# Layer 0 expert tiles: a row's weight, shift and scale chosen on GpSimd in six instructions instead of on VectorE in five

## The chip, the cores and the metric

The kernel runs on one core of one Trainium2 chip. The metric is the device time of one execution in microseconds (us). The time of the kernel before is the median of three runs, 3926.92 us (3926.24 to 3932.78).

## The reference, cut to what matters

The network has two layers. Each is a token mixer (attention with a top-k mask in layer 0, four selective scans in layer 1) followed by a mixture of experts. The change lies in the mixture of experts of layer 0, where each of the 4 x 1024 tokens goes to two of eight experts:

```python
def _moe(tokens, router_w, w1, b1, w2, b2):
    probs = jax.nn.softmax(logits, axis=-1)
    rw, re = jax.lax.top_k(probs, TOP_K)
    rw = rw / jnp.maximum(rw.sum(-1, keepdims=True), 1e-12)
    combine = jnp.zeros((N, E), tokens.dtype).at[jnp.arange(N)[:, None], re].set(rw)
    out = tokens
    for e in range(E):
        h = jax.nn.gelu(tokens @ w1[e] + b1[e], approximate=False)
        y = h @ w2[e] + b2[e]
        out = out + combine[:, e:e + 1] * y
    return out
...
t = _to_tokens(x)
t = t + _L0_ffn_ref(_ln_t(t), ...)
```

The tokens are normalized (`_ln_t`), so the sum for a token is its raw row, plus its normalized row, plus the two experts' results, each times its weight.

## The kernel before, in words

Attention runs first, image by image (about 0 to 1955 us in the profile). As an image is finished, its tokens are routed, and each row of 256 channels is written twice into `slots_x0`, a DRAM buffer with a region for each expert. A row carries five more numbers: at position C (256) the number of its first expert, at C + 1 and C + 2 what gives its weight, at C + 3 the shift and at C + 4 the scale of its normalization.

Then come the layer 0 tiles (about 1955 to 2193 us): 36 tiles of 256 rows, each for one expert. The loop `for i in range(USUAL)` calls seven steps for each tile, in this order:

- `load` (L1442 to L1447): SyncE's DMA queue fetches the rows `xs` (6 buffers) and the expert's weights `w1` and `w2` (4 buffers).
- `normed` (L1454, L1456): `xn`, the normalized rows, two halves of 128. In tiles 0 to 13 GpSimd makes both; from tile 14 on VectorE makes the first half and ScalarE the second.
- `small` (L1470 to L1481): VectorE copies the expert's two biases out of a table at an offset in a register (`b1e`, `b2e`). It then makes three pairs of numbers for the 256 rows. `best` is 1 where the row's first expert is the tile's expert. `wt`, the row's weight, is best times one number plus another. `shift` is best times the row's shift. In the end `best` is overwritten with (scale + 1) times best. Each of these tiles has 2 buffers.
- `turned` (L1463, L1465): TensorE transposes `xn` into `tp` (one PSUM buffer), VectorE copies it to `xe`.
- `hidden` (L1488, L1490): TensorE multiplies by `w1` into `hp` (2 PSUM buffers), ScalarE applies Gelu and the bias and writes `hid`.
- `result` (L1496, L1499): TensorE multiplies by `w2` into `yp` (one PSUM buffer), VectorE adds the bias and writes `ys` (8 buffers).
- `store` (L1503, L1505, L1507): ScalarE makes ys times `wt` plus `shift` in place, VectorE adds the raw row times `best`, and GpSimd starts the DMA that writes the tile to `rows_y0`. In this way the one tile that belongs to a token's first expert also brings its raw and its normalized row.

After each tile, other work is issued six steps at a time (the list `beside`). From tile 14 on this is `whole(0)`: 16 gathers on GpSimd (L1918), which fetch each token's two results from the rows of tiles 0 to 14 (`FIRST` is 15) and add them; they are issued beside tiles 14, 15 and 16. After a pause come their transposes, and then layer 1's first preparation: the normalization (L1805 to L1835), the projections (L1841, L1863) and the step sizes (L1857 to L1892), and `lead`, which has one GpSimd product over 1024 columns (L1958). From tile 22 on `whole(1)` gathers image 1 in the same way (`SECOND` is 23).

No order is written out by hand in this part, unlike in the attention and in the scans, which stand under `manual_schedule`. Here the compiler puts the instructions of each engine into an order of its own, from the code's order, the data that each needs and the buffers that it has to wait for. What is then in an engine's queue is issued in that order. `small` of a tile follows `normed` in the code and stands ahead of the tile's matmuls and of what is issued beside that tile. The buffers tie it to the tile two before: `wt` and `shift` are free again when L1503 of that tile has read them, the last factor when L1505 has.

Of the kernel before, what the change touches and what calls it, by code (L numbers as in the profile page):

```python
# [11 lines left out]
F32 = mybir.dt.float32  # L12
# [5 lines left out]
ALU = mybir.AluOpType  # L18
# [3 lines left out]
P = 128  # L22
B = 4
C = 256
# [15 lines left out]
T = 256  # L40
# [25 lines left out]
def metaformer(ctx: ExitStack, tc: tile.TileContext, t: dict, out: bass.AP):  # L66
    nc = tc.nc
# [120 lines left out]
    every_expert = cons.tile([P, NTILE], F32, tag="every_expert", name="every_expert")  # L188
# [1226 lines left out]
    def tiles_of_0(st, name):  # L1415
# [7 lines left out]
        pb = st.enter_context(tc.tile_pool(name=f"{name}_b", bufs=2))  # L1423
# [5 lines left out]
        class Tile0:  # L1429
# [37 lines left out]
            def small(self):  # L1467
                e = self.register(0, E - 1, [mybir.EngineType.DVE])
                self.b1e = pb.tile([P, CT], F32, tag="b1e", name="b1e")
                nc.vector.tensor_copy(self.b1e, b1[:, bass.ds(e, 1)].rearrange("p o c -> p (o c)"))  # L1470
                self.b2e = pb.tile([P, C], F32, tag="b2e", name="b2e")
                nc.vector.tensor_copy(self.b2e, b2[:, bass.ds(e, 1)].rearrange("p o d -> p (o d)"))
                self.best = pb.tile([P, T // P], F32, tag="best", name="best")
                nc.vector.tensor_scalar(self.best, self.xs[:, :, C], every_expert[:, self.i : self.i + 1], None,
                                        ALU.is_equal)
                self.wt = pb.tile([P, T // P], F32, tag="wt", name="wt")
                nc.vector.tensor_tensor(self.wt, self.best, self.xs[:, :, C + 1], ALU.mult)
                nc.vector.tensor_tensor(self.wt, self.wt, self.xs[:, :, C + 2], ALU.add)
                self.shift = pb.tile([P, T // P], F32, tag="shift", name="shift")
                nc.vector.tensor_tensor(self.shift, self.best, self.xs[:, :, C + 3], ALU.mult)  # L1480
                nc.vector.scalar_tensor_tensor(self.best, self.xs[:, :, C + 4], 1.0, self.best, ALU.add, ALU.mult)  # L1481

            def hidden(self):
                hp = ps_h.tile([P, CT, T], F32, tag="hp", name="hp")
# [16 lines left out]
            def store(self):  # L1501
                for a in range(T // P):
                    nc.scalar.activation(self.ys[:, a], self.ys[:, a], AF.Identity, bias=self.shift[:, a : a + 1],  # L1503
                                         scale=self.wt[:, a : a + 1])
                    nc.vector.scalar_tensor_tensor(self.ys[:, a], self.xs[:, a, :C], self.best[:, a : a + 1],  # L1505
                                                   self.ys[:, a], ALU.mult, ALU.add)
                nc.gpsimd.dma_start(rows_y0[ts(self.i, T)].rearrange("(a p) c -> p a c", p=P), self.ys)  # L1507

# [456 lines left out]
    with ExitStack() as st:  # L1965
        Tile0, pb, ps_n = tiles_of_0(st, "m0")
# [282 lines left out]
    with ExitStack() as st:  # L2249
        pb = st.enter_context(tc.tile_pool(name="m1_b", bufs=2))  # L2250
# [267 lines left out]
```

## Time and profile before

| | us |
|---|---|
| median of three runs | 3926.92 |
| the profiled execution | 3942.8 |
| its span, from the first to the last instruction | 3940.7 |
| TensorE (PE) busy in the span | 3366.7 |
| VectorE (DVE) busy | 3044.7 |
| ScalarE (ACT) busy | 2779.1 |
| GpSimd (POOL) busy | 1969.6 |
| GpSimd's gathers L1918 between 1955 and 2195 us (the 32 of images 0 and 1) | 41.0 |
| GpSimd's stores L1507, 36 of them | 29.7 |
| GpSimd's normalization L1456, 28 halves | 17.9 |

The profile is of one execution, which took 15.9 us longer than the median. In its groups, a row names the line, the engine, the operation, the tile written and the tiles read, with their shapes; then the busy time and the mean duration in ns, and after the next bar the idle time ahead of these instructions. In a timeline a row has the start and the duration in us, then the instruction, and in brackets how long its engine had been idle before it and what it had waited for. Where several instructions are merged into one row, an x and their number stand at its end. PE's matmul ends are modelled, and spans on GpSimd are rough.

### The profile page before, as it was taken

To read this page: it belongs to the slowest core of one execution; us is meant where nothing else is said; L and a number is where in the kernel's file an instruction comes from. 1 tells how busy PE (TensorE), PEld (TensorE's weight loads), DVE (VectorE), ACT (ScalarE), POOL (GpSimd) and SP (SyncE) were. 2 spreads that over 40 slices of the span, in tenths; PEclk is the share of its full clock that TensorE was granted. 3 is DMA by queue.
4 is the path that set the end of the run, shared out by engine and by line. 5 is a ranking of instruction groups with operands and counts; after the bars stand their busy time and mean duration, and the time that the engine had idled before them with its cause. 6 is when DMAs were issued, how large, how long until landed. Compare 5 with 4: busy or idle time off the path is not lost. (4 is left out here: it accounts for less than half of the span.)

```text
span 3940.7 us, 49978 instructions
## 1 busy us (share of the span) xinstructions
PE 3366.7 (85%) x17139; PEld 1891.0 (48%) x17186; DVE 3044.7 (77%) x5283; ACT 2779.1 (71%) x3756; POOL 1969.6 (50%) x1796
## 2 busy tenths in 40 slices
PE   8378888888888888886688889998998989998998
PEld 5134444534344444543375433443443433687887
DVE  3689898998989898989476789999999999331113
ACT  2889999899989999997244677767767777322223
POOL 0145544585647564675443576556556558213112
PEclk9567887788778787787798999999999999999999
DMA  9400084000000000000275344334334334556666
GB/s 294 111 1 1 1 233 126 1 1 25 17 1 1 1 28 6 1 12 12 80 230 158 127 126 129 125 106 131 121 106 131 124 106 150 162 182 195 198 205 232
DMA packets 279802, 393.74 MB, mean 100 GB/s; under 512 B 80368, under 2 KB 221424, under 8 KB 279408
## 3 DMA queue, kind: packets, MB, share of 16 engines
q1 hardware_dynamic: 253824, 333.73, 27.7%
q0 software_dynamic: 21216, 53.73, 4.2%
q10 hardware_dynamic: 4496, 2.97, 0.2%
q8 instruction: 138, 2.26, 0.2%
q14 instruction: 128, 1.05, 0.1%
HBM read 280.41 MB, written 109.94 MB: 99 GB/s over the span
## 5 line engine op out<-in xcount | busy, mean ns | idle before, releaser
L828 POOL TENSOR_SCALAR dr<-s_n,last 128x1024 bf16<-128x1024 f32 x250 | 719.0, 2892 | 735.2 <-DVE state L856 377.1
L738 ACT ACTIVATE junk_a<-s_n,state 128x1024 int8<-128x1024 f32 x448 | 514.7, 1149 | 23.8 <-DVE low L859 6.5
L2114 POOL TENSOR_TENSOR da_c<-prod,come 128x1024 f32<-128x1024 f32 x128 | 257.7, 2013 | 369.6 <-DVE h L2120 321.8
L742 DVE TENSOR_SCALAR_CACHE_REDUCE junk_v<-s_n,state 128x1024 int8<-128x1024 f32 x320 | 408.7, 1277 | 8.8
L2314 ACT ACTIVATE hid<-hp,b 128x256 f32<-128x256 f32 x288 | 120.2, 470 | 350.0 <-issue 231.0
L789 DVE SCALAR_TENSOR_TENSOR w<-s_n,win 128x1024 f32<-128x1024 f32 x256 | 350.3, 1369 | 5.3
L2323 DVE TENSOR_TENSOR ys<-yp,b2e 128x512 f32<-128x512 f32 x36 | 24.9, 692 | 383.8 <-PE yp L2320 383.8
L792 DVE MAX8 win<-w 128x8 f32<-128x1024 f32 x256 | 314.5, 1228 | 8.8
L2125 PE MATMUL sum<-h,ident 128*128 128x512 f32 x512 | 264.1, 640 | 56.7 <-DVE h L2120 52.9
L896 ACT ACTIVATE ex<-sT 128x1024 f32<-128x1024 f32 x256 | 247.0, 1016 | 91.7 <-PE sT L888 91.7
L2103 DVE TENSOR_TENSOR_SCAN sum<-da,uu 128x1024 f32<-128x1024 f32 x127 | 289.6, 2280 | 27.5 <-PE sum L2085 13.9
L2079 POOL TENSOR_TENSOR uu<-dx,bb 128x1024 f32<-128x1024 f32 x127 | 303.6, 2391 | 1.7 <-DMA bb<-bc_d 1.7
L738 ACT ACTIVATE junk_a<-s_n,guess 128x1024 int8<-128x1024 f32 x256 | 294.3, 1150 | 7.2
L2096 DVE TENSOR_TENSOR_SCAN h<-da,uu 128x1024 f32<-128x1024 f32 x127 | 287.9, 2267 | 1.0 <-POOL uu L2079 1.0
L2120 DVE TENSOR_TENSOR_SCAN h<-da_c,uu 128x1024 f32<-128x1024 f32 x127 | 288.3, 2270 | 0.0
L2091 PE MATMUL sum<-da_c,ident 128*128 128x512 f32 x512 | 257.1, 626 | 33.1 <-POOL da_c L2114 29.0
L906 PE MATMUL o_ps<-ex,vT 128*32 128x256 f32 x2048 | 236.9, 450 | 51.4 <-ACT ex L896 36.7
L2325 POOL DMA_INDIRECT results<-ys,to x72 | 70.2, 974 | 415.0 <-DVE ys L2323 359.8
L2063 ACT ACTIVATE da_c<-delta,a_log 128x1024 f32<-128x1024 f32 x128 | 269.5, 2106 | 5.2 <-DMA rows_y<-ys 5.2
L2310 PE MATMUL hp<-xe,w 128*128 128x256 f32 x1152 | 259.9, 384 | 8.9 <-ACT hid L2314 5.3
L2320 PE MATMUL yp<-w2e,hid 128*128 128x256 f32 x1152 | 257.8, 382 | 11.3 <-issue 11.3
L772 ACT COPY s_n<-sp 128x1024 f32<-128x1024 f32 x256 | 245.2, 1003 | 19.1 <-PE sp L764 11.5
(796 smaller groups left out, 7568.8 us busy)
## 6 DMA issues: line engine op xcount, KB each, us to landing
cb<-bc_d SPq DMA_DIRECT2D x128, 512.0 KB
bb<-bc_d SPq DMA_DIRECT2D x127, 512.0 KB
w<-in_w SPq DMA_DIRECT2D x36, 1024.0 KB
w2e<-in_w SPq DMA_DIRECT2D x36, 1024.0 KB
slots_x<-zeros SPq DMA_DIRECT2D x1, 33669.0 KB
slots_x<-zeros SPq DMA_DIRECT2D x1, 33282.0 KB
w<-in_w SPq DMA_DIRECT2D x72, 256.0 KB
xs<-slots_x SPq DMA_DIRECT2D x36, 261.0 KB
```

The source lines that it names most:

```text
L738: nc.scalar.activation(junk, self.row(r), AF.Sign, bias=thr, scale=-1.0, accum_out=u)
L742: nc.vector.tensor_scalar(junk, self.row(r), thr, None, ALU.is_lt, ALU.add, accum_out=u)
L789: nc.vector.scalar_tensor_tensor(w, self.row(r), self.win[:, r, 0:1], self.row(r), ALU.is_gt if r < LAST_DVE else ALU.is_ge, ALU.subtract, ...
L792: nc.vector.max(out=self.win[:, r, 1:], in_=w)
L828: ins = eng.tensor_scalar(dr, self.row(r), self.last[:, r : r + 1], None, ALU.is_lt)
L2063: nc.scalar.activation(grid(self.da_c), cols_flipped(self.prep.delta[:, self.c]), AF.Exp, scale=self.decay)
L2079: nc.gpsimd.tensor_tensor(self.uu[:, 0], self.prep.dx[:, self.c], self.bb, ALU.mult)
L2096: nc.vector.tensor_tensor_scan(rows.rearrange("p r w -> p (r w)"), self.da, self.uu[:, 0], 0.0, ALU.mult, ALU.add)
L2103: nc.vector.tensor_tensor_scan(self.sum[:, ::-1], self.da[:, ::-1], self.uu[:, 0][:, ::-1], 0.0, ALU.mult, ALU.add)
L2120: nc.vector.tensor_tensor_scan(self.hs, self.da_c, self.uu[:, 1], 0.0, ALU.mult, ALU.add)
L2125: nc.tensor.matmul(cols_flipped(self.sum[:, ts(h, HALF)]), ident, grid(self.hs)[:, :, ts(h, half)], start=False, stop=False)
L2310: nc.tensor.matmul(hp[:, i], self.w1[:, c, ts(2 * r + i, P)], self.xe[:, c], start=(c == 0), stop=(c == CT - 1))
```

## The change

The three values of a row are made by GpSimd. The comparison, the two operations for `wt` and the one for `shift` are the same, on another engine. The last one, (scale + 1) times best, is made in two operations, scale times best and then plus best, and goes to a tile of its own, `scale`, also with 2 buffers; L1505 reads it instead of `best`. The two bias copies stay on VectorE. `best` is now read by GpSimd alone.

```diff
@@ small
-                self.best = pb.tile([P, T // P], F32, tag="best", name="best")
-                nc.vector.tensor_scalar(self.best, self.xs[:, :, C], every_expert[:, self.i : self.i + 1], None,
+                pool = nc.gpsimd.tensor_tensor
+                self.best, self.wt, self.shift = (pb.tile([P, T // P], F32, tag=n, name=n) for n in ("best", "wt", "shift"))
+                nc.gpsimd.tensor_scalar(self.best, self.xs[:, :, C], every_expert[:, self.i : self.i + 1], None,
                                         ALU.is_equal)
-                self.wt = pb.tile([P, T // P], F32, tag="wt", name="wt")
-                nc.vector.tensor_tensor(self.wt, self.best, self.xs[:, :, C + 1], ALU.mult)
-                nc.vector.tensor_tensor(self.wt, self.wt, self.xs[:, :, C + 2], ALU.add)
-                self.shift = pb.tile([P, T // P], F32, tag="shift", name="shift")
-                nc.vector.tensor_tensor(self.shift, self.best, self.xs[:, :, C + 3], ALU.mult)
-                nc.vector.scalar_tensor_tensor(self.best, self.xs[:, :, C + 4], 1.0, self.best, ALU.add, ALU.mult)
+                pool(self.wt, self.best, self.xs[:, :, C + 1], ALU.mult)
+                pool(self.wt, self.wt, self.xs[:, :, C + 2], ALU.add)
+                pool(self.shift, self.best, self.xs[:, :, C + 3], ALU.mult)
+                self.scale = pb.tile([P, T // P], F32, tag="scale", name="scale")
+                pool(self.scale, self.best, self.xs[:, :, C + 4], ALU.mult)
+                pool(self.scale, self.scale, self.best, ALU.add)
@@ store
-                    nc.vector.scalar_tensor_tensor(self.ys[:, a], self.xs[:, a, :C], self.best[:, a : a + 1],
+                    nc.vector.scalar_tensor_tensor(self.ys[:, a], self.xs[:, a, :C], self.scale[:, a : a + 1],
                                                    self.ys[:, a], ALU.mult, ALU.add)
```

The same functions serve a rare branch with more tiles than usual (`more_tiles`); the profile shows none of it.

## The prediction

> **What bounds the kernel now.** I read the page first (busy shares, then the chain of work that ended last), then the stage of the layer 0 tiles by itself: busy time by stretches, groups of instructions, waits, and the timeline of all engines and of GpSimd alone. The chain on the page starts at 2190.36 us with the last store of a layer 0 tile (2.55 us to land); the loads of the next stage follow it. So the end of this stage, 1955 to 2193 us, is on the path, and each microsecond that it grows or shrinks reaches the end. Inside it:
>
> ```profile
> 1980.00:2018.00 38.00, 35.95 (x172) 28.97 (x171) 28.64 (x103) 15.87 (x33) 18.72 (x27) 1.00 0.79 235
> 2018.00:2055.00 37.00, 31.57 (x148) 24.86 (x147) 25.18 (x86) 17.38 (x37) 13.08 (x14) 1.00 0.76 222
> 2055.00:2080.00 25.00, 22.88 (x112) 17.85 (x111) 19.96 (x64) 12.12 (x25) 16.34 (x15) 1.00 0.99 282
> ...
> 2120.00:2150.00 30.00, 17.84 (x67) 13.41 (x66) 25.42 (x58) 17.41 (x23) 5.16 (x4) 0.78 0.37 117
> ```
>
> The columns after the length are the busy times of PE, PE's weight loads, VectorE (DVE), ScalarE (ACT) and GpSimd (POOL). Up to 2080 us TensorE is the fullest (35.95 of 38 us, 22.88 of 25); only from 2120 to 2150 us does VectorE lead, with 25.42 of 30 us. Tiles 3 to 9 come every 4.34 us, tiles 10 to 20 every 4.82 us (two in 9.63).
>
> The five operations that the change takes from VectorE:
>
> ```profile
> L1474 DVE TENSOR_SCALAR best<-xs,every_expert 128x2 f32<-128x2 f32 x36 | 9.1, 251 | 0.2
> L1477 DVE TENSOR_TENSOR wt<-best,xs 128x2 f32<-128x2 f32 x36 | 8.6, 238 | 0.8
> L1478 DVE TENSOR_TENSOR wt<-wt,xs 128x2 f32<-128x2 f32 x36 | 5.7, 158 | 0.0
> L1480 DVE TENSOR_TENSOR shift<-best,xs 128x2 f32<-128x2 f32 x36 | 5.7, 159 | 0.0
> L1481 DVE SCALAR_TENSOR_TENSOR best<-xs,best 128x2 f32<-128x2 f32 x36 | 6.1, 170 | 0.0
> ```
>
> Together 35.2 us in 36 tiles, 0.98 us for a tile. Their own waits are about 1 us in all, and none of the large waits of the stage names them: ScalarE waits 69.8 us for the matmuls of hp, and VectorE itself waits 33.1 us for the matmuls of yp. They fill gaps.
>
> GpSimd's queue, in its own order:
>
> ```profile
> 2039.70 0.72 POOL L1507 DMA_DIRECT2D rows_y<-ys  x1 [2.89 <-DVE ys L1505]
> 2043.43 1.05 POOL L1918 DMA_INDIRECT y<-rows_y,slot  x1 [3.00 <-DMA rows_y<-ys]
> ...
> 2052.74 1.38 POOL L1507 DMA_DIRECT2D rows_y<-ys  x1
> ...
> 2061.72 0.79 POOL L1507 DMA_DIRECT2D rows_y<-ys  x1
> ...
> 2068.53 1.53 POOL L1918 DMA_INDIRECT y<-rows_y,slot  x1 [0.30 <-issue]
> 2069.50 3.54 POOL L1507 DMA_DIRECT2D rows_y<-ys  x4
> ```
>
> L1507 stores a tile's result; L1918 are 16 gathers of image 0. The first gather waits for the store of tile 14 (2039.70). From there to 2070.06 us the queue is gathers, with only the stores of tiles 15 and 16 among them; the stores of tiles 17 to 20, whose data was ready from 2057.25 us on, come out together at 2069.50. Nobody needed them: ys has 8 buffers. Tile 17 in the other queues:
>
> ```profile
> 2045.80 0.21 DVE L1474 TENSOR_SCALAR best<-xs,every_expert 128x2 f32<-128x2 f32 x1
> ...
> 2054.90 0.29 DVE L1472 COPY b2e<-b 128x256 f32 x1
> ...
> 2055.90 0.45 ACT L1490 ACTIVATE hid<-hp,b1e 128x256 f32<-128x256 f32 x1
> ...
> 2056.40 1.56 PE L1496 MATMUL yp<-w,hid 128*128 128x256 f32 x6 [0.27 <-ACT hid L1490]
> ```
>
> VectorE chose tile 17's values at 2045.80, when tile 15 had let go of the two buffers. ScalarE uses wt and shift at 2054.90; one hid further on in the same queue, TensorE is waiting (0.27 us) for ScalarE.
>
> **What the Trainium skill says.** (1) "Perfetto Trace Analysis", section Tensor Engine Instruction (MATMUL, LD_WEIGHTS): ACT, DVE and GpSimd are strict FIFO. The trace agrees: the four stores that waited until 2069.50. (2) "SBUF — State Buffer", section Who interferes with whom: a VectorE instruction with two SBUF inputs and a GpSimd one that reads SBUF exclude each other, and the later one is fully blocked. The trace agrees:
>
> ```profile
> 2136.44 2.56 POOL L1958 TENSOR_TENSOR lead_uu<-dx,held 128x1024 f32<-128x1024 f32 x1 [9.63 <-ACT ys L1503]
> 2136.70 2.31 DVE L1477 TENSOR_TENSOR wt<-best,xs 128x2 f32<-128x2 f32 x1
> ```
>
> The 128x2 product, 0.16 us elsewhere, took 2.31 us beside GpSimd's 2.56 us. (3) "TensorE: Matmul & The Clock Gate", Part 1: after some 3.4 us of idling TensorE runs at half rate and needs about as long to come back. Here, after 4.22 us idle before 2129.88, four matmuls took 2.08 us instead of 1.13.
>
> **The change, part by part.**
>
> Removed from VectorE: five instructions a tile. Where TensorE leads they gain nothing: TensorE's stream covers them, and VectorE waits for it. Where VectorE leads (2134.87 to 2144.47, when TensorE sat 6.42 us waiting for xe L1465) they count. The 2.31 us stall seems the prize, but the next instruction is the second product of L1505, with two SBUF inputs too: it would wait for the same GpSimd operation until 2139.00. Left are shift 0.07, wt and best 0.14, best 0.14: 0.35 us, and some 0.3 us each in the first tile and between 2072 and 2080. I take -1 us. Bounds: 0 and, if VectorE paced tiles 17 to 30, 14 x 0.98 = -13.7 us.
>
> Added to GpSimd: six 128x2 operations. The nearest rows are 128x8:
>
> ```profile
> 834.92 0.20 POOL L313 TENSOR_TENSOR space<-space,x 128x8 f32<-128x8 f32 x1
> 835.08 0.21 POOL L314 TENSOR_TENSOR x<-space,x 128x8 f32<-128x8 f32 x1
> 835.38 0.26 POOL L315 TENSOR_SCALAR x<-x 128x8 f32<-128x8 f32 x1
> ```
>
> In that run of eight, L308 to L316, starts lie 0.27 us apart on average (833.75 to 835.61); with 0.29 for dependent ones six take 1.7 us. In tiles 3 to 9 GpSimd does 1.36 (xn) + 0.75 (store) = 2.1 us in 4.34; with 1.7 it is 3.8. They are ready after L1505 of two tiles before, the result is needed 6.9 us later (1990.60 to 1997.51), and xn follows at 1993.31 after the store ended at 1991.65: they fit exactly into that hole. Cost 0; bounds 0 and 0.3 us a tile, 2 us in all, if they push xn. The sixth operation is there as (x + 1) times best is made in two. What they block on VectorE lies in its gaps: 0, at most 0.22 us a tile from tile 17 on, 4 us (beside GpSimd's xn the two of L1505 take 1.09 us instead of 0.87).
>
> Moved, and this decides: the six operations go into the queue that holds the gathers. No order is written by hand for these tiles; the compiler orders each queue by what it believes ready, and code order among those. That is read off GpSimd's rows: the durations of the gathers (five short, four long, three short, four long) show that only the ninth went ahead of its place, and the stores of tiles 15 and 16 stand nearly where the code has them. Tile 17's wt and shift can't be written before L1503 of tile 15 (2044.24) and its scale not before L1505 of tile 15 (2045.42), both after the first gather (2043.43); and in the code all 16 gathers, issued beside tiles 14 to 16, come before tile 17. So tile 17's six operations stand behind gather 16: 2070.06 + 4 x 0.29 (best, two for wt, shift) = 2071.2, against 2054.90 now. ScalarE's queue stands there for up to 16.3 us, with tile 18's hid behind it, and TensorE behind hid. Less if some slip in before gather 14 (2064.4): 10.7 us. I take 15. Nothing hides it: the 8 buffers of ys covered the stores, but wt, shift and scale have two, and it's ScalarE's own queue that stands.
>
> TensorE then idles 15 us and restarts at half rate: four matmuls cost 0.95 us more at 2129.88, some 2 us until the clock is back. +2, bounds 0 and 4.
>
> The same at the second 16 gathers (2090.51 to 2116.39, beside tiles 22 to 24): tile 25's operations come after them and a store of about 0.9: 2117.3 + 1.2 = 2118.5, needed at 2113.84. +4.6; ScalarE has other work near there and VectorE leads soon after, so I take +3, bounds 0 and 4.6.
>
> Sum: -1 + 15 + 2 + 3 = +19 us. The profiled execution took 3942.8 us (span 3940.7 and 2.1 around it), 15.9 above the median of 3926.92. On it the change gives 3961.8; the same difference on the median gives 3946. What is late next is every tile from 18 on; TensorE paces them, so nothing is caught up.
>
> **Rivals.** R1, the operations get ahead of the gathers, or the gathers are ordered later. For it: tile 17's best needs no buffer of tile 15, and the compiler does move things. Against: seven gathers stand before tile 15's store. Then only the -1 remains: 3926. R2, faster: GpSimd's queue does no harm and VectorE was the true pace. Place: tiles 17 to 30, 2055 to 2165 us; price 0.98 us a tile, 13.7 us; it decides once xe L1465 and ys L1499 start on the end of a VectorE instruction instead of that of a matmul. For it: 25.42 of 30 us from 2120 on, and 14.3 us of TensorE's waits are for xe. Against: in the other stretches VectorE starts ys right at yp's end. 3913. R3, the compiler foresees the wait and puts tile 18's hid ahead of tile 17's L1503, which halves the stall: +9, 3936.
>
> **How the numbers follow.** About 0.2% (7.9 us) can be told from no change, so "same" is 3919 to 3934.8. Forecast 3946: 0.58, its own range 3937 (10.7 - 1) to 3958 (16.3 + 4 + 4.6 + 2 + 4). R3 3936: 0.08, slower. R1 3926: 0.20, same. R2 3913: 0.14, faster. Slower 0.66, same 0.20, faster 0.14. The range reaches from the upper part of R2 to the forecast's upper end: 3918 to 3958.
>
> **What would show it.** Right: on GpSimd, tile 17's operations start after the last of the first 16 gathers; a wait of L1503 for GpSimd of 10 us or more, a hole of that length in TensorE near 2056 to 2071 with half clock after it, and a smaller one near the second 16. VectorE's five rows gone, and the 2 us stall handed to L1505. Wrong: those operations among or before the gathers, tile spacing of 4.34 and 4.82 us unbroken, or a spacing that shrinks by 1 us from tile 17 on.

## The result, and the profile after

The changed kernel takes 3948.20 us (median of six runs, 3941.07 to 3951.28), the kernel before in the same comparison 3926.58 us: the ratio on record is 1.0061, 95% interval 1.0048 to 1.0075 (the two medians alone give 1.0055). A second comparison on another occasion, in which both kernels ran 11 to 13 us slower, gave 1.0047 (1.0035 to 1.0059). The forecast was 3946 us. The profiled execution after took 3951.28 us with a span of 3949.4.

The two profiled spans differ by 8.7 us only, because the profiled run of before was itself 16 us above its median, and tile 4's `xe` starts anywhere from 1971.39 to 1988.86 us in the profiled runs shown here. So I compare the stage by itself: from the start of tile 4's `xe` copy on VectorE to that of tile 35, read off VectorE's timeline. It took 194.19 us before and 212.90 after, 18.7 us more; a second profile of the changed kernel gave 212.76. This **stretch** is the measure from here on.

The busy time by stretches of the changed kernel, with the columns that the prediction names; behind them stand the TensorE clock that was granted, the DMA share and GB/s:

```profile
1980.00:2018.00 38.00, 35.67 (x174) 29.27 (x173) 24.45 (x58) 16.82 (x35) 30.18 (x79) 1.00 0.79 239
...
2055.00:2080.00 25.00, 5.72 (x29) 4.36 (x27) 4.57 (x11) 3.58 (x9) 20.38 (x26) 0.67 0.65 153
2080.00:2120.00 40.00, 37.85 (x177) 29.11 (x178) 23.87 (x53) 15.46 (x31) 22.09 (x47) 0.91 0.53 159
```

Before, TensorE filled 22.88 of the 25 us from 2055 to 2080; now it has 5.72, ScalarE 3.58, VectorE 4.57. Only GpSimd is busy (20.38). In what follows the hole is this idle time of TensorE. In the first row GpSimd has 30.18 where it had 18.72, VectorE 24.45 where it had 28.64, and TensorE is as full as before (35.67 against 35.95). GpSimd's queue around the hole:

```profile
2045.01 0.76 POOL L1508 DMA_DIRECT2D rows_y<-ys  x1 [0.85 <-DVE b1e L1470]
2045.80 0.21 POOL L1481 TENSOR_TENSOR scale<-best,xs 128x2 f32<-128x2 f32 x1
2046.09 0.20 POOL L1482 TENSOR_TENSOR scale<-scale,best 128x2 f32<-128x2 f32 x1
2046.38 0.38 POOL L1475 TENSOR_SCALAR best<-xs,every_expert 128x2 f32<-128x2 f32 x1
2047.54 0.20 POOL L1477 TENSOR_TENSOR wt<-best,xs 128x2 f32<-128x2 f32 x1 [0.78 <-ACT ys L1504]
...
2049.16 1.10 POOL L1919 DMA_INDIRECT y<-rows_y,slot  x1 [1.12 <-issue]
...
2054.07 0.79 POOL L1508 DMA_DIRECT2D rows_y<-ys  x1
...
2067.45 0.78 POOL L1508 DMA_DIRECT2D rows_y<-ys  x1
...
2074.22 1.55 POOL L1919 DMA_INDIRECT y<-rows_y,slot  x1 [0.31 <-issue]
2075.21 0.79 POOL L1481 TENSOR_TENSOR scale<-best,xs 128x2 f32<-128x2 f32 x1
2075.36 0.78 POOL L1477 TENSOR_TENSOR wt<-best,xs 128x2 f32<-128x2 f32 x1
...
2076.24 0.49 POOL L1478 TENSOR_TENSOR wt<-wt,xs 128x2 f32<-128x2 f32 x1
```

The store at 2045.01 is tile 14's, the scale after it (two operations) tile 16's, `best` tile 18's, and the `wt` at 2047.54 tile 17's. Then come 16 gathers with two stores among them, and only behind the last gather tile 17's scale (2075.21) and tile 18's `wt` (2075.36 and 2076.24). The other engines:

```profile
2076.61 0.89 DVE L1506 SCALAR_TENSOR_TENSOR ys<-xs,scale,ys 128x256 f32<-128x256 f32 x2 [18.02 <-POOL scale L1482]
...
2078.58 1.09 ACT L1504 ACTIVATE ys<-ys,shift,wt 128x256 f32<-128x256 f32 x2 [19.88 <-POOL wt L1478]
...
2080.08 2.08 PE L1489 MATMUL hp<-xe,w 128*128 128x256 f32 x4 [18.96 <-ACT hid L1491]
```

VectorE stood 18.02 us for scale of tile 17, ScalarE 19.88 for tile 18, TensorE 18.96 for the `hid` that is queued behind ScalarE's L1504. ScalarE's wait is put down to `wt`, which was written by 2076.73; what came last was tile 18's L1500 (2077.82, 0.68 us), and that was queued behind VectorE's own wait. So two queues stood side by side. The same again, smaller, at the second gathers, for scale of tile 25:

```profile
2137.30 0.89 DVE L1506 SCALAR_TENSOR_TENSOR ys<-xs,scale,ys 128x256 f32<-128x256 f32 x2 [5.55 <-POOL scale L1482]
```

The six operations and VectorE's five rows: the rows at L1474 to L1481 are gone from VectorE, and in their place stand

```profile
L1475 POOL TENSOR_SCALAR best<-xs,every_expert 128x2 f32<-128x2 f32 x36 | 13.0, 373 | 3.0 <-POOL scale L1482 0.2
L1477 POOL TENSOR_TENSOR wt<-best,xs 128x2 f32<-128x2 f32 x36 | 12.3, 341 | 53.0 <-ACT ys L1504 52.9
L1478 POOL TENSOR_TENSOR wt<-wt,xs 128x2 f32<-128x2 f32 x36 | 8.0, 221 | 0.0
L1479 POOL TENSOR_TENSOR shift<-best,xs 128x2 f32<-128x2 f32 x36 | 12.3, 342 | 0.0
L1481 POOL TENSOR_TENSOR scale<-best,xs 128x2 f32<-128x2 f32 x36 | 9.6, 277 | 0.8
L1482 POOL TENSOR_TENSOR scale<-scale,best 128x2 f32<-128x2 f32 x36 | 10.1, 283 | 2.4
```

### The profile page after: what moved, and what is told of

Same layout as the page of the kernel before. It is cut to its first block, busy times and chain, and to the rows that moved or that the text cites. A ratio compares the mean times of both kernels' runs of the same rounds, so it can differ in the third digit from the quotient of the medians.

```text
span 3949.4 us, 50067 instructions
## 1 busy us (share of the span) xinstructions
PE 3355.5 (85%) x17139; PEld 1888.7 (48%) x17186; DVE 3024.6 (77%) x5103; ACT 2779.3 (70%) x3756; POOL 2023.1 (51%) x2012
## 4 chain that ended last, share of the span: by engine, by line
PE 38%; DVE 28%; ACT 14%; issue 9%; POOL 8%; DMA 1%; another core or an unknown queue 0%; SPq 0%; DVEq 0%; POOLq 0%; ACTq 0%
ACT junk_a L738 8%; PE hp L2311 6%; PE yp L2321 6%; DVE junk_v L742 4%; PE sum L2092 4%; DVE w L789 4%; DVE win L792 3%; DVE sum L2104 3%; ACT s_n L772 3%; PE o_ps L906 2%; DVE h L2121 2%; ACT ex L896 2%; DVE yc L2131 2%; DVE h L2097 2%; POOL dr L828 2%
## 5 line engine op out<-in xcount | busy, mean ns | idle before, releaser
L2092 PE MATMUL sum<-h,twice 128*128 128x512 f32 x512 | 247.7, 607 | 12.1 <-DVE sum L2104 12.1
```

The lines of the kernel that those rows point to most:

```text
L2092: nc.tensor.matmul(self.sum[:, ts(h, HALF)], ident if eye is None else eye, view[:, ts(h, HW // NHALF), :], start=False, stop=last)
```

## The experiments

All stretches are from tile 4 to tile 35, in us; "by 19", "22" and "23" is how far the tiles had come since tile 4 when that tile's `xe` started; "25 to 26" is the step that holds the second stall. Ratios are to the kernel before in the same comparison, with the 95% interval.

| kernel | by 19 | by 22 | by 23 | 25 to 26 | stretch | ratio |
|---|---|---|---|---|---|---|
| before | 71.68 | 85.53 | 99.09 | 9.36 | 194.19 | 1 |
| after | 69.04 | 103.63 | 115.62 | 13.64 | 212.90 | 1.0061 (1.0048 to 1.0075) |
| after, again | 69.04 | 103.54 | 115.52 | 12.73 | 212.76 | 1.0047 (1.0035 to 1.0059) |
| VectorE in both stretches | 69.31 | 84.25 | 102.51 | 9.27 | 195.26 | 1.0011 (1.0001 to 1.0021) |
| VectorE in the first | 69.32 | 84.24 | 103.21 | 13.17 | 201.22 | 1.0014 (1.0005 to 1.0024) |
| VectorE in the second | 69.04 | 103.73 | 115.76 | 9.27 | 208.78 | 1.0026 (1.0015 to 1.0037) |
| five operations left out | 68.86 | 83.35 | 103.04 | 9.26 | 195.68 | (other data later) |
| six beside, unread | 71.69 | 85.62 | 99.00 | 9.29 | 194.00 | 0.9995 (0.9985 to 1.0005) |
| eight buffers | 68.95 | 90.01 | 104.50 | 9.26 | 199.18 | 1.0015 (1.0005 to 1.0025) |
| scale on VectorE | 69.00 | 103.17 | 115.15 | 11.88 | 215.21 | 1.0045 (1.0030 to 1.0060) |
| three gathers a tile | 76.86 | 96.50 | 108.48 | 9.27 | 202.61 | 1.0028 (1.0016 to 1.0040) |
| GpSimd in tiles 0 to 15 | 69.33 | 84.89 | 102.82 | 9.27 | 197.50 | 1.0015 (1.0004 to 1.0025) |
| the same, transposes later | 69.31 | 83.96 | 89.02 | 23.93 | 191.39 | 0.9994 (0.9981 to 1.0006) |
| before, transposes later | 71.51 | 84.36 | 91.12 | 22.50 | 192.49 | 1.0002 (0.9989 to 1.0015) |

Where the transposes come later, other work lies between tiles 25 and 26, so that column says nothing there.

**Is it the gathers, or the operations?** Three runs give the values back to VectorE in chosen tiles only (the edit shown has both ranges of tiles, the other two runs have one each):

```diff
-                nc.gpsimd.tensor_scalar(self.best, ...)
+                eng = nc.vector if 16 <= self.i < 22 or 24 <= self.i < 30 else nc.gpsimd
+                eng.tensor_scalar(self.best, ...)
...
+                if eng is nc.vector:
+                    eng.scalar_tensor_tensor(self.scale, self.xs[:, :, C + 4], 1.0, self.best, ALU.add, ALU.mult)
```

> The six operations stay on GpSimd except in tiles 16 to 21 and 24 to 29, where VectorE makes the values in five. Theory Q (the loss comes only where the operations stand behind the 16 gathers): both stalls go, 18.7 us of hole (less the 3 us that the tiles before gained) and some 4 us at the second gathers, so 3922 to 3928 us, within 0.2% of the kernel before; no wait of ScalarE for GpSimd over 2 us. Rival S (the six operations cost a little in every tile: they push xn, or GpSimd and VectorE block each other): 12 of 36 tiles are changed back, so a third of the 21.6 us returns: 3941 us.

> VectorE makes the values in tiles 16 to 21 only (beside the first 16 gathers); elsewhere GpSimd. Theory Q: the large hole goes, the small one at the second gathers stays: 3948 less 16 to 20 gives 3928 to 3932 us. Rival S: 6 of 36 tiles, a sixth of 21.6 us: 3944.6 us.

> VectorE makes the values in tiles 24 to 29 only (beside the second 16 gathers); elsewhere GpSimd. Theory Q: the large hole of about 18.7 us stays, the small one goes: 3948 less 3 to 5 gives 3943 to 3945 us. Rival S: 3944.6 us, so the time doesn't tell them apart here, the trace does: under Q the hole in TensorE from about 2061 to 2080 us stays whole and tile 26's xe isn't late against tile 25's any more. The savings of this run and of the run with the first stretch only should add up to that of the run with both, if the two stalls are independent.

Both: stretch 195.26, 17.6 us below the changed kernel, as theory Q has it; under rival S a third of the loss, 6 us, would have come back. The time was 5.2 us above the kernel before in its comparison (3928.17 against 3922.93; by the interval 0.4 to 8.2), a little more than I had expected. At tile 24, VectorE waited 6.1 us for GpSimd's late scale, since the two engines share the buffers at the hand-over. First only: 201.22, 11.7 us below, and the time, 3928.27, as expected. Second only: 208.78, 4.1 us below, and the hole stays (TensorE 19.4 us for `hid`). 11.7 + 4.1 is 15.8 of 17.6; taken in the other order they are 13.5 (208.78 - 195.26) and 6.0 (201.22 - 195.26). So the first stall costs 11.7 to 13.5 us net, the second 4 to 6. The third run's time missed my 3943 to 3945: 3931.09 against 3922.93, 8.2 us above the kernel before (by the interval 5.9 to 14.5), where the stretch says 14.6. What made up the rest lies outside the stretch, and I did not find it.

**What is it worth to take the work from VectorE?**

```diff
+                if not first:
+                    first.append([pb.tile([P, T // P], F32, tag=n, name=n, bufs=1) for n in ("best", "wt", "shift")])
...
+                self.best, self.wt, self.shift = first[0]
```

> The kernel before, with the five operations on VectorE made for the first tile of the loop only; all later tiles use that tile's weight, shift and scale, so the values chosen are left out of the work. It measures what taking the five operations from VectorE is worth when nothing is given to another engine. Forecast's term: -1 us, and after the trace of the changed kernel (3.2 us gained by tile 19) up to -4: 3922 to 3926 us. Rival (VectorE paces the tiles, 0.98 us each from tile 17 on): -13.7 us, 3913 us.

The time (3973.88 us) can't be used: other values go into layer 1, and its work changes with them. The stretch can: 195.68, 1.5 us longer than before, not shorter. The tiles were 2.8 us ahead by tile 19 and 2.2 by tile 22; at tile 23 they were 4.0 behind. The rival of 13.7 us is out. What took the lead back stands in the waits of the stage, here of the kernel before and then of the kernel with GpSimd in tiles 0 to 15 (engine and line, what was waited for, us in total, times, longest):

```profile
PE op L1931 <- DMA y<-rows_y,slot: 0.2, 1, 0.2
```

```profile
PE op L1935 <- DMA y<-rows_y,slot: 3.9, 3, 1.6
```

`op` are the transposes of image 0's gathered rows, which TensorE has queued among the tiles. Before, they come when the gathers are there (0.2 us); where the tiles run ahead, TensorE waits for them: 3.9 us here, 5.0 with the five operations left out, 3.7 and 4.4 in the first two runs above. Three runs test that, and with it the half of the change that no gather touches:

```diff
-                nc.gpsimd.tensor_scalar(self.best, ...)
+                eng = nc.vector if self.i >= 16 else nc.gpsimd
+                eng.tensor_scalar(self.best, ...)
...
-            yield from pause(24)
+            yield from pause(24 if b else 30)
```

> GpSimd makes the values in tiles 0 to 15 only, VectorE from tile 16 on: the half of the change that no gather touches. Theory Q: no wait for GpSimd over 2 us; 2 to 3 us are gained by tile 19 and lost at tile 23, where TensorE's transposes of image 0 wait 8 to 11 us for gathers (0.6 us in the kernel before): stretch 194.5 to 196.5 us, time within 0.2% of the kernel before. Rival S (the six operations cost something in every tile, here 16 of 36): 4 to 10 us slower.

> The same, with image 0's transposes issued one tile later (a pause of 30 in place of 24 steps, image 0 only). If it is the wait of those transposes for the gathers that eats what VectorE gains, that wait falls below 3 us and the gain stays: stretch 190 to 193 us, 1 to 4 us below the kernel before. Rival: what follows the transposes (image 0's norm and preparation, for which tile 29 waits some 20 us) is late by the same tile, and the gain is lost there: 194 to 198 us.

> The control: the kernel before with image 0's transposes one tile later and nothing else. They wait only 0.6 us for gathers there, so at most that can be gained: stretch 193.5 to 197 us, no change in time that can be told. If it gains 2 us or more, the gain of the run with GpSimd in tiles 0 to 15 is the later transposes' own and not VectorE's.

The "8 to 11" and "0.6" us in the first of these are a sum of two rows, the matmuls' and their weight loads', which wait for the same thing; the matmuls' own are 3.7 to 5.0 and 0.2. The first run's stretch of 197.50 is 1.0 above what I expected; 2.4 us were gained by tile 19 and 3.7 were missing at tile 23. With the transposes one tile later that wait is gone, and the stretch is 191.39, 6.1 us shorter, as the theory had it. But the control gains too: 192.49, 1.7 us below the kernel before, where I had expected 0.6 at most (193.5 or more). What is left for VectorE's relief, here in the first 16 tiles only, is 1.1 us of stretch. In time, neither version can be told from the kernel before (0.9994 and 1.0002): none beats it.

**Is it the wait for the values, or GpSimd's load?** VectorE as before, and GpSimd makes the six operations too, into a tile that nobody reads:

```diff
+                spare = pb.tile([P, 4, T // P], F32, tag="spare", name="spare")
+                p_best, p_wt, p_shift, p_scale = (spare[:, n] for n in range(4))
+                nc.gpsimd.tensor_scalar(p_best, self.xs[:, :, C], every_expert[:, self.i : self.i + 1], None, ALU.is_equal)
+                pool(p_wt, p_best, self.xs[:, :, C + 1], ALU.mult)
...
```

> VectorE makes the values as in the kernel before, and GpSimd executes the six operations of the change too, into a spare tile that nobody reads. Theory Q (only the wait for results that stand behind the gathers costs): no engine waits for GpSimd, so the time is that of the kernel before within 3 us, and the stretch from tile 4 to tile 35 is 194 to 197 us. Rival S (GpSimd's own time, or VectorE blocked by it, costs): some 10 us or more above the kernel before.

194.00 and 0.9995: the operations themselves cost nothing that can be told. What costs is the wait for their results.

**How much depends on the place in the queue?**

> The changed kernel once more, on the same chip as the others of this group, as their measure: 18 to 22 us above the kernel before, and in its trace the same 18 to 19 us hole in TensorE and a stretch from tile 4's xe to tile 35's of about 213 us (before: 194 us).

It came 19.5 us above the kernel before, with a stretch of 212.76 and a hole of 18.95 us. The runs below are held against it. Two of them change the place in the queue; the first gives the values eight buffers:

```diff
-                self.best, self.wt, self.shift = (pb.tile([P, T // P], F32, tag=n, name=n) for n in ("best", "wt", "shift"))
+                few = pb.tile([P, 4, T // P], F32, tag="few", name="few", bufs=8)
+                self.best, self.wt, self.shift, self.scale = (few[:, n] for n in range(4))
```

> The change, with wt, shift, scale and best packed in one tile of eight buffers in place of two each. GpSimd's operations are then free to go ahead as soon as a tile's xs is there, and by the order of its queue those up to tile 19 stand before the first 16 gathers (with two buffers: up to tile 16 or 17), those up to tile 27 before the second 16. Theory Q: tile 20 is then the first to wait, two or three tiles of 4.8 us later, so the hole of 18.7 us shrinks to about 5 to 9 and is hidden in part by the wait of image 0's transposes for the gathers; the second stall goes. 12 to 17 us below the changed kernel, stretch 196 to 201 us. If the buffers didn't matter (rival: GpSimd's load itself), the time stays at that of the changed kernel.

199.18 against 212.76, and 14.1 us below the changed kernel in the same comparison: as expected. The wait of ScalarE that stays, in this kernel's waits, and who waits for ScalarE:

```profile
DVE ys L1506 <- ACT ys L1504: 11.5, 12, 6.4
...
ACT ys L1504 <- POOL few L1479: 11.0, 2, 7.7
...
PE yp L1497 <- ACT hid L1491: 7.7, 4, 6.6
```

ScalarE waits 7.7 us at the longest, now at tile 20, where it was 19.9, and 25 to 26 takes 9.26 again: the second stall is gone. The second way keeps the two buffers and lets the gathers in by threes:

```diff
-            yield from fetched(b, y, range(NHALF))
-            yield from pause(24)
+            for _ in fetched(b, y, range(NHALF)):
+                yield
+                yield
+            yield from pause(8)
```

> The change, with three gathers issued beside a tile in place of six, and the pause before image 0's transposes shortened by as much. In GpSimd's queue scale of tile 17 then stands behind 10 of the first 16 gathers (before: 16), wt of tile 18 behind 13, wt of tile 19 behind all. Theory Q: each wait is as long as the gathers ahead of it, so scale of tile 17 comes some 9 us earlier and wt of tile 18 some 5 us; the hole of 18.7 us shrinks by about 5 us. Since a part of the hole lies where TensorE would wait for the gathers of image 0 anyway, the stretch from tile 4 to tile 35 shrinks by less: 208 to 212 us (changed kernel: 212.8). If the place in the queue didn't matter, the hole stays at 18 to 19 us.

VectorE's wait for scale of tile 17 fell to 8.3 us (from 18.0, as worked out), ScalarE's for `wt` of tile 18 to 12.6, and TensorE's largest waits were 6.7 and 3.4 us. At tile 22 that was worth 7.1 us, more than the 5 I gave it. The stretch, 202.61, missed my 208 to 212: I had left out that the second gathers are spread too, and there the stall went (9.27 from tile 25 to 26, 4.4 less than 13.64).

**Which of the two waits holds the tiles?** Only scale goes back to VectorE:

```diff
-                pool(self.scale, self.best, self.xs[:, :, C + 4], ALU.mult)
-                pool(self.scale, self.scale, self.best, ALU.add)
+                nc.vector.scalar_tensor_tensor(self.scale, self.xs[:, :, C + 4], 1.0, self.best, ALU.add, ALU.mult)
```

> Only scale goes back to VectorE (one operation for two); best, wt and shift stay on GpSimd. VectorE's wait of 18.0 us for tile 17's scale is then gone, ScalarE's of 19.9 us for tile 18's wt stays. If either wait alone is enough to stop the tiles (theory Q with two stalls side by side): the hole stays at 15 to 18 us and the time within 4 us of the changed kernel. If VectorE's wait is the one that counts (rival): the hole goes to under 8 us and the time falls by 10 us or more.

```profile
DVE scale L1481 <- POOL best L1475: 20.1, 2, 16.9
ACT ys L1503 <- POOL wt L1478: 18.5, 1, 18.5
```

The hole stayed (TensorE 17.5 us for `hid`), the time too (1.0045 beside 1.0047). But the run doesn't separate the waits: VectorE's new operation reads `best`, which GpSimd makes behind the gathers as well, so VectorE stood 16.9 us all the same. Two of the runs above tell more. With eight buffers ScalarE's wait stands alone: VectorE's longest there, 6.4 us, is for ScalarE and not for GpSimd, and TensorE still stood 6.6 us for `hid`. With three gathers a tile VectorE's wait ended 6 us before ScalarE's: TensorE's 6.7 us ended with `xe`, which VectorE copies, and the 3.4 us after it with `hid`, which stood behind ScalarE's L1504. So either wait is enough to stop TensorE. How much of the 18.96 us each would have cost alone is not shown.

## Why the prediction was right

The sum was 19 us and the stretch grew by 18.7. The mechanism is the forecast one, and three points came as they were put. Three terms of the sum were off, and their errors cancel: where -1 stood, +1.1 is left; 15 + 2 was 11.7 to 13.5, and 3 was 4 to 6. That the sum comes within 0.3 us is luck; that the gathers in GpSimd's queue cost more than anything else, and about how much, is not.

- **Cost of the six operations: right.** GpSimd's groups above add up to 65.3 us for 36 tiles, 1.8 us a tile by the durations listed, some of which overlap (1.7 forecast, from starts). They fit in, though not all in the hole between store and `xn`: three stand behind `xn` ahead of the store, three behind the store. Tiles 5 to 12 come every 4.34 us in both kernels (the prediction had this pace end at tile 9), and the run with unread operations shows no cost.
- **First stall: right in kind, and one step of it failed.** "Tile 17's wt and shift can't be written before L1503 of tile 15 (2044.24) ... both after the first gather (2043.43)": in the changed kernel the first gather came later, 60.3 us after tile 4's `xe` and not 58.9, tile 15's L1504 ended earlier, at 58.6 us and not 59.8, and tile 17's `wt` and `shift` got out at 2047.54, before it. What stood behind was tile 17's scale and tile 18's `wt`. I counted ScalarE's wait alone; VectorE's wait for scale came as well, and ScalarE's fell on tile 18. The hole was 18.96 us, above my upper bound of 16.3.
- **"TensorE paces them, so nothing is caught up": wrong.** Where nothing stalls first (VectorE in both stretches), the tiles take 18.26 us from tile 22 to 23, as the transposes wait for the gathers (17.93 with GpSimd in tiles 0 to 15, where VectorE has no such wait at a hand-over); after the hole only 11.99, as the gathers have landed meanwhile. About 6.3 us of the first stall lie where TensorE would have lost time anyway, so it costs 11.7 to 13.5 us net, where my two terms (15 + 2) had 17.
- **Half clock: right.** The first four matmuls after the hole took 2.08 us; the granted clock was 0.50 from 2080 to 2083.5 us and 1.00 from 2087 to 2092. With three gathers a tile, four took 2.08 and 2.07 us after the waits of 6.7 and 3.4 us. From tile 20 to 22 the changed kernel needs 12.81 us, with VectorE in both stretches 10.82: +2.0, as forecast.
- **Second stall: too small.** +3, at most 4.6, was the forecast; the runs give 4 to 6. The place was as forecast, tile 25 behind the second gathers, but again it was scale, at the end of the chain, that came last: VectorE waited 5.55 us (2137.30).
- **VectorE's relief: wrong sign in the stretch.** -1 was forecast; with the five operations left out it is +1.5, since the 2.2 us of lead are lost to the gathers at tile 23. Only with the transposes moved are 1.1 us left of it, from 16 of the tiles. That refutes rival R2 (13.7 us). R1 came true for tile 17's `wt` and `shift` and not for its scale, which was enough for the hole; that the hole isn't halved refutes R3.
- **The 2.31 us stall is handed on: right.** Beside `lead_uu` the two products of L1506 now take 2.96 us in place of 0.9:

```profile
2160.98 2.73 POOL L1959 TENSOR_TENSOR lead_uu<-dx,held 128x1024 f32<-128x1024 f32 x1 [8.58 <-DVE dx L1892]
2161.41 2.96 DVE L1506 SCALAR_TENSOR_TENSOR ys<-xs,scale,ys 128x256 f32<-128x256 f32 x2
```

With the sizes from the runs: 1.1 for what is left when both stalls are gone (195.26 - 194.19), 11.7 to 13.5 for the first stall, 6.0 to 4.1 for the second; either pair adds 17.6, together 18.7 us. The time rose by 21.6 us in one comparison and 19.5 in the other. By their intervals the rise is 18.8 to 29.4 and 13.8 to 23.2 us, so the stretch's 18.7 lies just under the first and inside the second; what a remainder of 1 to 3 us would be is open.

The Trainium skill's page "Perfetto Trace Analysis", section GPSIMD Engine Instruction, advises to time GpSimd by the spacing of starts and not by the durations shown. This case agrees: behind the last gather (2074.22, listed with 1.55 us) tile 17's scale starts at 2075.21, inside it, and is listed with 0.79 us, while the next three starts follow 0.15 to 0.16 us apart.

## What to carry to other kernels

Before a small operation moves to another engine, list what else that engine's queue holds, and for how long; what decides is not its 0.2 us but the 26 us of gathers that it may stand behind, and whether anyone needs its result meanwhile. Count every result of the moved group, the last one made too: here tile 17's `wt` slipped in ahead of the gathers and its scale did not. More buffers put the operations ahead in the queue and took over two thirds of the loss away; and a stall that falls where the stage would wait anyway costs less than its length.

## What the runs showed of the hardware

GpSimd is held up by VectorE as well, not only the other way round. Beside a scan of 2.28 us on VectorE, one 128x2 product on GpSimd took 2.06 us, 0.20 elsewhere (at 2046.09), and GpSimd's next operation started only 2.16 us after this one's start:

```profile
2169.22 2.28 DVE L1957 TENSOR_TENSOR_SCAN lead_cum<-inner,delta 128x1024 f32<-128x1024 f32 x1
2169.43 2.06 POOL L1482 TENSOR_TENSOR scale<-scale,best 128x2 f32<-128x2 f32 x1
```

The Trainium skill's page "SBUF — State Buffer", section Who interferes with whom, has it as a lock of which the later one waits; the trace shows it in both directions within 10 us, here and at 2161.41 above.
